# Two attention layers, layer 0: the softmax totals of two head groups made in one visit to TensorE

## Chip, cores and metric

The kernel runs on one core of one Trainium2 chip. The metric is device time in microseconds (us). A comparison uses medians of several runs; the profile is one further execution of the same program.

## What is computed

The input is `x` with shape (8, 512, 32, 32): 8 batch elements, 512 channels, 1024 positions. There are two layers; each normalizes its input by groups of channels and adds an attention block to it. The change is in layer 0 alone:

```python
def _L0_conv_ref(x, gn_w, gn_b, qkv_w, qkv_b, proj_w, proj_b):
    ...                                   # group norm -> normed (b, c, t)
    qkv = jnp.einsum('oc,bct->bot', qkv_w, normed) + qkv_b[None, :, None]
    q, k, v = jnp.split(qkv, 3, axis=1)
    ...                                   # 8 heads of 64 channels, q and k scaled
    weight = jnp.einsum('bct,bcs->bts', q, k)
    weight = jax.nn.softmax(weight.astype(jnp.float32), axis=-1).astype(q.dtype)
    a = jnp.einsum('bts,bcs->bct', weight, v).reshape(b, c, t)
    out = jnp.einsum('oc,bct->bot', proj_w, xf + a) + proj_b[None, :, None]
    return out.reshape(b, -1, h, w)

x = x + _L0_conv_ref(_gn(x), ...)         # layer 0
x = x + _L1_conv_ref(_gn(x), ...)         # layer 1: mixes heads, normalizes the softmax
```

All arithmetic is in fp32. The softmax is made without a maximum: the exponentials `e` are multiplied with `v`, their totals are made on the side, and the product is multiplied with the reciprocals of the totals at the end.

## The kernel before

**Stages.** Layer 0 handles one batch element after the other, up to about 1750 us; layer 1 fills the rest. For each batch element there is an attention loop (some 115 us) and then four projections of 24 us each or less (`k`, `v` and `q` of the next element, the output of this one), each made of seven half-size products by `project0`.

**Groups and slots.** `attention0` works through 8 groups of a batch element. A group `g` is one pair of heads and one of the two blocks of 512 queries. Inside a group, 8 blocks of 128 keys follow, so the loop counter `i` runs over 64 steps, two at a time. For two steps TensorE makes the scores (L1086, into PSUM tile `s`, two buffers), ScalarE the exponentials (L1091, tiles `e`, seven buffers), TensorE the values of the two steps before (L1112, accumulating in the two PSUM tiles `a0` and `a1` of the group), and VectorE adds the exponentials into `zacc` (L1097 for the first addition of a group, L1099 for the others). Each scores or values block of two steps is sixteen matmul records in 64x64 tiles of the TensorE array.

**The end of a group.** After its eighth key block ScalarE copies the two accumulators out (L1123, `u`). Three further steps follow, placed by slot numbers: an `Agenda` is a table from a slot to functions, and the loop runs slots `i` and `i + 1` after the work of step `i`. What is still in the agenda after the loop is run by `ag.flush()`, which stands between the `k` and the `v` projection of the next element.

- `totals`, two slots after the group's end: four matmuls with a block of ones (L1131, tiles of 128x32, eight records) add `zacc` over the partitions into half of a PSUM bank `z`; ScalarE copies that half out (L1136, `row`), and the SP queue moves one row of each 32 to a compact tile `zc` (L1138).
- `reciprocals`, six slots after: VectorE adds the two `u` tiles (L1142), makes the reciprocals (L1145) and two checksums (L1155, L1159); SP writes the reciprocals to DRAM (L1147, `zd`) and reads them back, broadcast over partitions, in two transfers (L1150, `rzb`).
- `finish`, ten slots after: VectorE multiplies and adds into `xa` (L1166, L1168).

`z` takes its PSUM bank from the same tag `a0` (two buffers) that the group accumulators and the single banks of `project0` use.

**What else lies in the slots.** Slots 2 to 8 start `xa`, 4 to 19 hold statistics of the last output and weight combinations, 20 to 38 sums over the next element's channels on ScalarE, 43 and 45 two small matmuls for the group means and squares of the next element (L624, L635, 128x128 tiles), 47 their inverse root on VectorE, 49 to 61 the normalization of the next element on ScalarE, and 32 and 33 the loads of the next left factors. In the last batch element other work takes some of these places: the two small matmuls stand at slots 22 and 25.

**Order.** The program is scheduled by hand (`manual_schedule`): each engine executes in the order in which the code issues, and the SP queue likewise. The pools have fixed buffer counts; `zpool` has two of each tag unless a tile says otherwise, `stat` two.

**In `project0`** the first product goes to two single banks (`a0`), and the products `t6`, `t5`, `t7` to double banks (`s`, two buffers), so `t7` reuses the bank pair of `t6`, which VectorE frees at L933. The last product's two banks are freed by VectorE at L960 for `k` and `q`.

Of the kernel before, what the change touches and what calls it, by code (L numbers as in the profile page):

```python
# [9 lines left out]
F32 = mybir.dt.float32  # L10
# [8 lines left out]
P = 128  # L19
# [448 lines left out]
def tile_two_attention_layers(  # L468
# [19 lines left out]
    nc = tc.nc  # L488
    B, C, T = x_d.shape
# [4 lines left out]
    FB = 512  # L494
# [21 lines left out]
    def const_tile(name, shape, dt=F32):  # L516
        return const.tile(shape, dt, tag=name, name=name)
# [15 lines left out]
    ones = const_tile("ones", [P, P])  # L533
# [165 lines left out]
    with ExitStack() as l0:  # L699
# [4 lines left out]
        zpool = l0.enter_context(tc.tile_pool(name="zpool", bufs=2))  # L704
        stat = l0.enter_context(tc.tile_pool(name="stat", bufs=2))
        ps_s = l0.enter_context(tc.tile_pool(name="ps_s", bufs=2, space=PSUM))
        ps_a = l0.enter_context(tc.tile_pool(name="ps_a", bufs=1, space=PSUM))
# [4 lines left out]
        def score_psum(nm):  # L712
            return ps_s.tile([P, 2, FB], F32, tag="s", name=nm)
# [13 lines left out]
        HC = C // 2  # L727
# [10 lines left out]
        def left_tile(which, b):  # L738
            t = wpool.tile([P, 7, 2, HC], F32, tag="left", name=f"left_{which}_{b}")
            left_t[which] = t  # L740
            return t
# [5 lines left out]
        a21 = {}  # L747

        def load_blocks(which, queue=nc.sync, tag="u0"):

            t = left_tile(which, 0)
            if tag == "junk":
                a21[which] = zpool.tile([P, T], F32, tag=tag, name=f"a21_{which}", bufs=1)[
                    :, :C
                ].rearrange("p (k o) -> p k o", k=2)
            else:
                a21[which] = zpool.tile([P, 2, HC], F32, tag=tag, name=f"a21_{which}")
            for dst, i, j in (
                (t[:, 0], 0, 0), (t[:, 1], 0, 1), (a21[which], 1, 0), (t[:, 2], 1, 1),
            ):  # L760
                for k in range(2):
                    queue.dma_start(
                        out=dst[:, k],
                        in_=SOURCES[which][ts(2 * j + k, P), i * HC : (i + 1) * HC],
                    )
# [13 lines left out]

        load_blocks("k")  # L780
        load_blocks("v")


# [290 lines left out]
        def attention0(b, agenda):  # L1074
            q, k, v = q_t[b], k_t[b], v_t[b]
            e, acc, u, zacc, zc, rzb = {}, {}, {}, {}, {}, {}

            def scores(i):

                f, hp, kc = i // (NG * H // 2), i // NG % (H // 2), i % NG  # L1080
                ps = score_psum(f"s0_{b}_{i}")
                for c in range(2):
                    for m in range(2):
                        r = slice(m * D, m * D + D)
                        k0 = kc * P + c * D
                        nc.tensor.matmul(  # L1086
                            ps[c * D : c * D + D, m], k[r, hp, k0 : k0 + D], q[r, hp, ts(f, FB)],
                            start=True, stop=True,
                        )
                e[i] = epool.tile([P, 2, FB], F32, tag="e", name=f"e0_{b}_{i}")  # L1090
                nc.scalar.activation(e[i], ps, AF.Exp, scale=S0 * S0)  # L1091

            def sums(i):
                g, kc = i // NG, i % NG
                if kc == 1:
                    zacc[g] = zpool.tile([P, 2, FB], F32, tag="zacc", name=f"zacc_{b}_{g}")
                    nc.vector.tensor_add(zacc[g], e[i - 1], e[i])  # L1097
                elif kc > 1:
                    nc.vector.tensor_add(zacc[g], zacc[g], e[i])  # L1099

            def values(i):

                g, hp, kc = i // NG, i // NG % (H // 2), i % NG
                if kc == 0:
                    acc[g] = [
                        ps_a.tile([P, FB], F32, tag=f"a{a}", name=f"a0_{b}_{g}_{a}", bufs=2 - a)
                        for a in range(2)
                    ]
                for a in range(2):
                    rows = slice(a * D, a * D + D)  # L1110
                    for m in range(2):
                        nc.tensor.matmul(  # L1112
                            acc[g][a][m * D : m * D + D], v[rows, kc, ts(2 * hp + m, D)],
                            e[i][rows, m], start=(kc == 0), stop=(kc == NG - 1),
                        )
                if kc == NG - 1:

                    u[g] = [
                        zpool.tile([P, FB], F32, tag=f"u{a}", name=f"u_{b}_{g}_{a}")
                        for a in range(2)  # L1120
                    ]
                    for a in (1, 0):
                        nc.scalar.copy(u[g][a], acc[g][a])  # L1123

            def totals(g):


                HB = FB // 2
                z = ps_a.tile([P, FB], F32, tag="a0", name=f"z_{b}_{g}", bufs=2)[:, :HB]
                for c in range(4):  # L1130
                    nc.tensor.matmul(  # L1131
                        z[c * 32 : c * 32 + 32], ones[:, :32], zacc[g][:, c // 2, ts(c % 2, HB)],
                        start=True, stop=True, tile_position=(0, c * 32),
                    )
                row = zpool.tile([P, HB], F32, tag="row", name=f"row0_{b}_{g}")
                nc.scalar.copy(row, z)  # L1136
                zc[g] = stat.tile([P, T // P], F32, tag="zc", name=f"zc_{b}_{g}")
                nc.sync.dma_start(out=zc[g], in_=row[0::32])  # L1138

            def reciprocals(g):  # L1140

                nc.vector.tensor_add(u[g][0], u[g][0], u[g][1])  # L1142
                zs = zc[g]
                rz = stat.tile([P, T // P], F32, tag="rz0", name=f"rz_{b}_{g}")
                nc.vector.reciprocal(rz, zs)  # L1145
                zd = dram.tile([2, FB], F32, tag=f"zd0_{b}_{g}", name=f"zd0_{b}_{g}")
                nc.sync.dma_start(out=zd, in_=rz)  # L1147
                rzb[g] = zpool.tile([P, FB], F32, tag="rzb", name=f"rzb_{b}_{g}")
                for m in range(2):
                    nc.sync.dma_start(  # L1150
                        out=rzb[g][m * D : m * D + D], in_=zd[m].partition_broadcast(D)
                    )
                col = b * H + g
                junk = stat.tile([P, T // P], F32, tag="junk0", name=f"junkz_{b}_{g}")
                nc.vector.tensor_scalar(  # L1155
                    junk, zs, 1.0, 0.0, ALU.mult, ALU.add, accum_out=chk[:, 1, col : col + 1]
                )
                r2 = stat.tile([P, T // P], F32, tag="r20", name=f"r2_{b}_{g}")
                nc.vector.scalar_tensor_tensor(  # L1159
                    r2, rz, 1.0 / RZ_MAX, rz, ALU.mult, ALU.mult,  # L1160
                    accum_out=chk[:, 0, col : col + 1],
                )

            def finish(g):
                hp, f = g % (H // 2), g // (H // 2)
                nc.vector.tensor_mul(u[g][0], u[g][0], rzb[g])  # L1166
                dst = xa_t[b][:, hp, ts(f, FB)]
                nc.vector.tensor_add(dst, dst, u[g][0])  # L1168


            for i in range(0, NI + 2, 2):
                if i < NI:
                    scores(i)
                    scores(i + 1)
                if i >= 2:
                    for w in (i - 2, i - 1):
                        values(w)
                        sums(w)
                    if (i - 1) % NG == NG - 1:
                        g = (i - 1) // NG  # L1180
                        agenda.at(i + 2, lambda g=g: totals(g))
                        agenda.at(i + 6, lambda g=g: reciprocals(g))
                        agenda.at(i + 10, lambda g=g: finish(g))
                agenda.run(i)
                agenda.run(i + 1)

# [18 lines left out]
        for b in range(B):  # L1205
# [10 lines left out]
            if b < 3:  # L1216

                which = ("k1", "q1", "p1")[b]
# [9 lines left out]
            else:  # L1228
# [11 lines left out]
                for c in range(NCC):  # L1240
                    ag.at(49 + 4 * c, lambda c=c: normalize_to(n_t["1"][:, c], 0, c))
            attention0(b, ag)
            slot = NI + 2
            if more:
# [24 lines left out]
    with ExitStack() as l1:  # L1269
# [5 lines left out]
        zpool = l1.enter_context(tc.tile_pool(name="zpool1", bufs=1))  # L1275
        stat = l1.enter_context(tc.tile_pool(name="stat1", bufs=2))
        ps_a = l1.enter_context(tc.tile_pool(name="ps1_a", bufs=2, space=PSUM))
# [18 lines left out]
        HC = C // 2  # L1296
# [645 lines left out]
        for b in range(B):  # L1942
            more = b + 1 < B
            a = Attention1(b)
# [147 lines left out]
```

## Time and profile before

| | |
|---|---|
| median of 3 runs | 3967.3 us (3964.85, 3967.30, 3968.17) |
| the profiled execution's own time | 3964.89 us |
| its span, first to last instruction | 3963.1 us |
| TensorE clock granted, mean | 0.996 of full |
| TensorE busy | 3874.9 us, 98% |
| VectorE busy | 2769.6 us, 70% |
| ScalarE busy | 1971.4 us, 50% |
| `z` matmuls (L1131) | 512 records |
| `row` copies (L1136) | 64, 0.376 us mean |
| `zc` (L1138), `zd` (L1147), `rzb` (L1150) transfers | 64, 64, 128 |

How to read it: the span is what the trace covers, and the execution's own time is 1.8 us longer. Busy shares are means over both layers. A line such as "L1131 PE MATMUL z<-zacc,ones 128*32 128x256 f32 x8" names the line in the kernel, the engine, the operation, the tile written and those read, the shape of the TensorE tile, partitions times elements, and how many such records were merged; the two numbers ahead of it are the start and the length in us. An entry in square brackets is idle time of the engine just before, and what ended it. TensorE's weight loads have rows of their own (PEld) and overlap the matmuls.

### The profile page before, as it was taken

The numbers are of one execution on the slowest core, as the hardware profiler recorded it, in microseconds if no ns is written. First come the engines' busy times: TensorE is split into PE (matmuls) and PEld (weight loads), VectorE is DVE, ScalarE is ACT, GpSimd is POOL, SyncE is SP. The second block draws the span as 40 slices with busy tenths as digits, with TensorE's granted clock in tenths as the row PEclk, the third lists the DMA queues.
The fourth block names the chain that finished last, engine by engine and source line by source line (L and its number), as shares of the span: only waits on it lengthen the run. The fifth ranks groups of instructions, "written<-read, shape, count | busy, mean of one in ns | idle before, by whom it ended". The sixth has DMA issues, their size and how long they took to land.

```text
span 3963.1 us, 95453 instructions
## 1 busy us (share of the span) xinstructions
PE 3874.9 (98%) x41868; PEld 1823.7 (46%) x41868; DVE 2769.6 (70%) x3741; ACT 1971.4 (50%) x2431; POOL 141.2 (4%) x182
## 2 busy tenths in 40 slices
PE   8999999999999999999999999999999999999997
PEld 4353535344353535344544545545545445445454
DVE  4747475665757474856967958859768679588596
ACT  1726354453627172624716718538347267175284
POOL 0000000000000000000100100001001001000010
PEclk9999999999999999999999999999999999999998
DMA  3313131121121121216938839749568478397494
GB/s 121 123 48 117 47 118 46 55 73 65 55 72 68 61 76 48 89 49 173 230 114 208 211 104 237 198 119 236 158 158 220 134 192 226 98 229 191 124 226 124
DMA packets 249593, 519.09 MB, mean 131 GB/s; under 512 B 51024, under 2 KB 58192, under 8 KB 242512
## 3 DMA queue, kind: packets, MB, share of 16 engines
q1 hardware_dynamic: 241984, 500.08, 44.2%
q0 software_dynamic: 7184, 12.81, 1.5%
q8 instruction: 331, 5.42, 0.6%
q14 instruction: 94, 0.77, 0.1%
HBM read 197.16 MB, written 46.92 MB: 62 GB/s over the span
## 4 chain that ended last, share of the span: by engine, by line
PE 90%; DVE 5%; DMA 3%; ACT 1%; issue 1%; SPq 0%; ACTq 0%; DVEq 0%
PE s L1086 11%; PE a L1112 11%; PE a L1725 11%; PE s L1630 10%; PE m L1667 6%; PE pk_p L904 6%; PE pq_p L904 5%; PE pv L1456 5%; PE pv_p L904 5%; PE pp_p L904 5%; PE pq L1381 4%; PE pp L1381 4%; PE pk L1381 3%; DMA re<-raw 3%; DVE et L1695 1%; DVE bn L1709 1%
## 5 line engine op out<-in xcount | busy, mean ns | idle before, releaser
L1695 DVE STREAM_TRANSPOSE et<-e 128x2048 f32<-128x2048 f32 x256 | 589.5, 2303 | 100.0 <-ACT e L1680 99.0
L1725 PEld LDWEIGHTS a<-et,v 128*64 128x64 f32 x16384 | 510.8, 139 | 296.4 <-issue 273.4
L1709 DVE BATCH_NORM_STATS2 bn<-e 128x6 f32<-128x512 f32 x1024 | 635.1, 681 | 0.0
L1091 ACT ACTIVATE e<-s 128x1024 f32<-128x1024 f32 x512 | 497.2, 1026 | 233.8 <-PE s L1086 233.4
L1642 ACT COPY raw<-s 128x1024 f32<-128x1024 f32 x480 | 470.2, 1018 | 211.6 <-PE s L1630 179.0
L1680 ACT ACTIVATE e<-m 128x1024 f32<-128x1024 f32 x512 | 496.3, 1021 | 156.1 <-issue 56.3
L1725 PE MATMUL a<-et,v 128*64 128x64 f32 x16384 | 558.9, 225 | 11.2 <-DVE et L1695 7.8
L1099 DVE TENSOR_TENSOR zacc<-zacc,e 128x1024 f32<-128x1024 f32 x384 | 468.7, 1221 | 87.8 <-ACT e L1091 65.5
L1630 PE MATMUL s<-k,q 64*64 64x512 f32 x4096 | 515.2, 607 | 5.8 <-DVE q L1496 3.2
L1086 PE MATMUL s<-q,k 64*64 64x512 f32 x4096 | 490.1, 593 | 2.3 <-ACT e L1091 2.3
L1112 PE MATMUL a<-e,v 64*64 64x512 f32 x4096 | 484.1, 589 | 0.0
L1667 PE MATMUL m<-re,wmix 32*32 32x512 f32 x8192 | 311.0, 602 | 19.5 <-DMA re<-raw 16.5
L1112 PEld LDWEIGHTS a<-e,v 64*64 64x64 f32 x4096 | 156.7, 133 | 282.8 <-issue 282.2
L1086 PEld LDWEIGHTS s<-q,k 64*64 64x64 f32 x4096 | 147.9, 133 | 275.2 <-issue 240.5
L1630 PEld LDWEIGHTS s<-k,q 64*64 64x64 f32 x4096 | 127.8, 132 | 220.8 <-issue 87.1
L1456 PE MATMUL pv<-wv,y 128*128 128x512 f32 x480 | 214.3, 599 | 0.0
L1773 POOL DMA_DIRECT2D zd<-rz x96 | 52.5, 552 | 3508.2 <-DVE rz L1767 3506.0
L1741 ACT COPY q<-a 64x256 f32<-64x256 f32 x256 | 94.0, 367 | 148.3 <-PE a L1725 146.2
L1456 PEld LDWEIGHTS pv<-wv,y 128*128 128x128 f32 x480 | 88.6, 190 | 119.8 <-issue 106.5
L1667 PEld LDWEIGHTS m<-re,wmix 32*32 32x32 f32 x8192 | 68.8, 103 | 162.4 <-ACT raw L1642 69.3
L1462 DVE COPY v<-pv 128x512 f32<-128x512 f32 x30 | 20.7, 689 | 159.5 <-PE pv L1456 80.9
L1097 DVE TENSOR_TENSOR zacc<-e,e 128x1024 f32<-128x1024 f32 x64 | 78.3, 1223 | 55.9 <-ACT e L1091 55.9
(317 smaller groups left out, 3866.4 us busy)
## 6 DMA issues: line engine op xcount, KB each, us to landing
re<-raw SPq DMA_DIRECT2D x1024, 256.0 KB
left_q<-left_q SPq DMA_DIRECT2D x17, 1792.0 KB
left_p<-left_p SPq DMA_DIRECT2D x17, 1792.0 KB
left_k<-left_k SPq DMA_DIRECT2D x10, 1792.0 KB
x<-in_x_dram SPq DMA_DIRECT2D x32, 512.0 KB
rzb<-zd SPq DMA_DIRECT2D x128, 128.0 KB
x<-x SPq DMA_DIRECT2D x64, 256.0 KB
y<-x SPq DMA_DIRECT2D x32, 512.0 KB
```

Of the source, the lines that this page charges most:

```text
L904: nc.tensor.matmul(out, st, mv, start=start, stop=(k == 1), skip_group_check=True)
L1086: nc.tensor.matmul(ps[c * D : c * D + D, m], k[r, hp, k0 : k0 + D], q[r, hp, ts(f, FB)], start=True, stop=True,)
L1091: nc.scalar.activation(e[i], ps, AF.Exp, scale=S0 * S0)
L1112: nc.tensor.matmul(acc[g][a][m * D : m * D + D], v[rows, kc, ts(2 * hp + m, D)], e[i][rows, m], start=(kc == 0), stop=(kc == NG - 1),)
L1456: nc.tensor.matmul(ps[:, m], y_t[b][:, c, ts(2 * i + m, P)], w[:, c], start=(c == 0), stop=(c == NCC - 1),)
L1630: nc.tensor.matmul(ps[c * D : c * D + D, m], qo_t[b][r, p, hp, ts(c, D)], k_t[b][r, hp, ts(kh, FB)], start=True, stop=True,)
L1642: nc.scalar.copy(dst, ps)
L1667: nc.tensor.matmul(ps[a // 2][c * 32 : c * 32 + 32, a % 2].rearrange("p (r h k) -> p h r k", r=2, h=2), wmix[rows].rearrange("p g i -> p ( ...
L1680: nc.scalar.activation(e[:, :, 2 * h : 2 * h + 2].rearrange("p r a k -> p a r k"), ps[h].rearrange("p a (r k) -> p a r k", r=2), AF.Exp,)
L1695: nc.vector.transpose(self.et[p, u].rearrange("p kb (r st a) g q -> p st kb r (a g q)", r=2, st=2)[:, st], self.e[p, s].rearrange("p r a ( ...
L1709: nc.vector.bn_stats(self.bn[n][:, p % 2, s, a], e[:, :, a].rearrange("p r k -> p k r"))
L1725: nc.tensor.matmul(acc[two * D : two * D + D, s].rearrange("p (x q) -> p x q", q=4), v_t[b][:, kb, ts(g, D)], et[:, kb, :, g], start=(kb = ...
```

## The change

`totals` is called once for two groups, after the odd one, and makes eight matmuls in place of four: the even group's sums go to the left half of the PSUM bank, the odd group's to the right half. One ScalarE copy takes the whole bank to `row` (now one buffer of 512 columns instead of two of 256); two SP transfers make the two `zc`. `reciprocals` of both groups stand six slots after the odd group's end, `finish` of the even group ten and of the odd group twelve slots after it. So the sums of three groups and the values of three groups can be alive at a time: `zacc` and `u0` get a third buffer, `zc` four. The tile `a21` of the weight blocks shares the tag `u0` and gets the same number.

```diff
-                a21[which] = zpool.tile([P, 2, HC], F32, tag=tag, name=f"a21_{which}")
+                a21[which] = zpool.tile([P, 2, HC], F32, tag=tag, name=f"a21_{which}", bufs=3)
...
-                    zacc[g] = zpool.tile([P, 2, FB], F32, tag="zacc", name=f"zacc_{b}_{g}")
+                    zacc[g] = zpool.tile(
+                        [P, 2, FB], F32, tag="zacc", name=f"zacc_{b}_{g}", bufs=3
+                    )
...
-                        zpool.tile([P, FB], F32, tag=f"u{a}", name=f"u_{b}_{g}_{a}")
+                        zpool.tile([P, FB], F32, tag=f"u{a}", name=f"u_{b}_{g}_{a}", bufs=3 - a)
...
             def totals(g):
                 HB = FB // 2
-                z = ps_a.tile([P, FB], F32, tag="a0", name=f"z_{b}_{g}", bufs=2)[:, :HB]
-                for c in range(4):
-                    nc.tensor.matmul(
-                        z[c * 32 : c * 32 + 32], ones[:, :32], zacc[g][:, c // 2, ts(c % 2, HB)],
-                        start=True, stop=True, tile_position=(0, c * 32),
-                    )
-                row = zpool.tile([P, HB], F32, tag="row", name=f"row0_{b}_{g}")
+                z = ps_a.tile([P, FB], F32, tag="a0", name=f"z_{b}_{g}", bufs=2)
+                for i in range(2):
+                    for c in range(4):
+                        nc.tensor.matmul(
+                            z[c * 32 : c * 32 + 32, ts(i, HB)], ones[:, :32],
+                            zacc[g - 1 + i][:, c // 2, ts(c % 2, HB)],
+                            start=True, stop=True, tile_position=(0, c * 32),
+                        )
+                row = zpool.tile([P, FB], F32, tag="row", name=f"row0_{b}_{g}", bufs=1)
                 nc.scalar.copy(row, z)
-                zc[g] = stat.tile([P, T // P], F32, tag="zc", name=f"zc_{b}_{g}")
-                nc.sync.dma_start(out=zc[g], in_=row[0::32])
+                for i in range(2):
+                    t = zc[g - 1 + i] = stat.tile(
+                        [P, T // P], F32, tag="zc", name=f"zc_{b}_{g - 1 + i}", bufs=4
+                    )
+                    nc.sync.dma_start(out=t, in_=row[0::32, ts(i, HB)])
...
                         g = (i - 1) // NG
-                        agenda.at(i + 2, lambda g=g: totals(g))
-                        agenda.at(i + 6, lambda g=g: reciprocals(g))
-                        agenda.at(i + 10, lambda g=g: finish(g))
+                        if g % 2:
+                            agenda.at(i + 2, lambda g=g: totals(g))
+                            for j in range(2):
+                                agenda.at(i + 6, lambda g=g - 1 + j: reciprocals(g))
+                                agenda.at(i + 10 + 2 * j, lambda g=g - 1 + j: finish(g))
```

More of the change, by code (lines that the diff above doesn't have):

```diff
@@ L1128, in totals @@
                 HB = FB // 2
-                z = ps_a.tile([P, FB], F32, tag="a0", name=f"z_{b}_{g}", bufs=2)[:, :HB]
-                for c in range(4):
-                    nc.tensor.matmul(
-                        z[c * 32 : c * 32 + 32], ones[:, :32], zacc[g][:, c // 2, ts(c % 2, HB)],
-                        start=True, stop=True, tile_position=(0, c * 32),
-                    )
-                row = zpool.tile([P, HB], F32, tag="row", name=f"row0_{b}_{g}")
-                nc.scalar.copy(row, z)
-                zc[g] = stat.tile([P, T // P], F32, tag="zc", name=f"zc_{b}_{g}")
-                nc.sync.dma_start(out=zc[g], in_=row[0::32])
+                z = ps_a.tile([P, FB], F32, tag="a0", name=f"z_{b}_{g}", bufs=2)
[7 more added lines that the diff above has]
+                row = zpool.tile([P, FB], F32, tag="row", name=f"row0_{b}_{g}", bufs=1)
+                nc.scalar.copy(row, z)
+                for i in range(2):
+                    t = zc[g - 1 + i] = stat.tile(
+                        [P, T // P], F32, tag="zc", name=f"zc_{b}_{g - 1 + i}", bufs=4
+                    )
+                    nc.sync.dma_start(out=t, in_=row[0::32, ts(i, HB)])
             def reciprocals(g):
```

## The prediction

> **What bounds the kernel now.** I read the page's first part for the busiest engine, its fourth for the engine that the end hangs on, then the chain in order of time and the timeline around one `totals`.
>
> ```profile
> PE 3874.9 (98%) x41868; PEld 1823.7 (46%) x41868; DVE 2769.6 (70%) x3741; ACT 1971.4 (50%) x2431; POOL 141.2 (4%) x182
> ...
> PE 90%; DVE 5%; DMA 3%; ACT 1%; issue 1%; SPq 0%; ACTq 0%; DVEq 0%
> ```
>
> TensorE holds 90% of the chain. In layer 0's attention it holds all of it. From the chain (start, us, what):
>
> ```profile
> 196.90 1.72 PE a L1112 x16
> 198.61 1.72 PE s L1086 x16
> ...
> 202.62 1.88 PE s L1086 x16
> 204.49 1.72 PE a L1112 x16
> ```
>
> The rhythm is 1.72 us for sixteen matmul records. The gap ahead of 202.62 holds 16 `a` records (1.72) and a `totals` (0.57 by the same view: 202.62 - 202.05). The scores after it take 1.88, not 1.72. So one `totals` costs the path 0.57 + 0.16 = **0.73 us**, and the two starts in the timeline confirm it:
>
> ```profile
> 127.04 1.90 PE L1112 MATMUL a<-e,v 64*64 64x512 f32 x16
> ...
> 128.87 0.64 PE L1131 MATMUL z<-zacc,ones 128*32 128x256 f32 x8
> ...
> 129.44 1.95 PE L1086 MATMUL s<-q,k 64*64 64x512 f32 x16
> 129.57 0.37 ACT L1136 COPY row<-z 128x256 f32<-128x256 f32 x1 [1.08 <-PE z L1131]
> ...
> 131.21 1.90 PE L1112 MATMUL a<-e,v 64*64 64x512 f32 x16
> ```
>
> From 127.04 to 131.21 are 4.17 us; two undisturbed blocks are 3.44. The remainder is 0.73 again, and it is the same to 0.01 us at every `totals` inside the loop.
>
> How much of it is work? `z` streams 256 columns into four column tiles, twice (eight records). A 256-column record elsewhere in this trace (`v0`, chain: 24.44 us for 112 records) takes 0.216 us; four column tiles run at once here (their records start 7 ns apart), so two steps of four are 0.43 us. The other **0.30 us** is the change of tile shape: the first `z` starts 0.52 us after the last `a` where 0.41 would follow, and the steps just after each change are stretched.
>
> ScalarE and VectorE are not the limit there: between 141.8 and 156.2 us they are busy 12.03 and 11.86 of 14.40 us, TensorE all of it. The second place that matters is the flush after the attention, where the last group's totals stand between two projections:
>
> ```profile
> 235.52 0.64 PE L1131 MATMUL z<-zacc,ones 128*32 128x256 f32 x8
> 235.63 0.75 DVE L960 SCALAR_TENSOR_TENSOR k<-pk_p,qkvb,tmp 128x512 f32<-128x512 f32 x1 [0.96 <-PE pk_p L904]
> ...
> 236.43 7.17 PE L904 MATMUL pv_p<-left_v,n 128*128 128x256 f32 x32 [0.27 <-DVE k L960]
> ...
> 243.61 0.69 DVE L1166 TENSOR_TENSOR u<-u,rzb 128x512 f32<-128x512 f32 x1 [4.73 <-DMA rzb<-zd]
> ...
> 247.17 1.22 DVE L933 TENSOR_TENSOR tmp<-tmp,pv_p 128x1024 f32<-128x1024 f32 x1 [2.14 <-PE pv_p L904]
> ```
>
> The last two lines show VectorE standing still for a broadcast to land, and then taking up the projection's work at 247.17, on time.
>
> **What the Trainium skill says.** "TensorEngine Tiling (Array Packing)", Key Properties: changing the tiling mode drains TensorE. The trace agrees: 0.30 us per visit from 64x64 tiles to 128x32 and back. "ScalarE: Activation LUTs", What ACT_TABLE_LOAD costs: an activation is a fixed part plus 0.833 ns an element, so one copy of 512 is cheaper than two of 256. The trace agrees: 0.373 us for 256 (L1136), 0.586 for 512 (L928). "DMA: Bandwidth & Descriptors", Latency and other measured facts: a DMA has a fixed cost near 2 us. The trace: `zc`, issued at 236.62 us, is read at 238.47, 1.85 us later.
>
> **The change, part by part.**
>
> 1. *Totals inside the loop.* Groups 0 to 5 of each of 8 batches: six visits become three, of 16 records each. A visit costs 0.73 for the first eight records and x for the next eight. x is not in the trace. Its floor is the streaming, 0.43; its ceiling is 0.48, if each step keeps the 0.24 us between the first two steps of `z` today. Under 0.43 it can't go, the columns being the same. I take 0.43, since scores also stretch only their first step (0.46, then 0.41). Gain: 24 pairs x (0.73 - 0.43) = **-7.2 us** (-6.0 at the ceiling).
>
> 2. *Groups 6 and 7.* Group 6's visit in the loop (0.73) goes away; both are made in the flush. There TensorE already waits: after `z` it resumes at +0.91 us, when VectorE's last `k` piece frees a bank, and without that wait would resume at +0.57. Eight more records move +0.57 to +1.00, so 0.34 of their 0.43 lies under the wait. Gain per batch 0.73 - 0.09 = 0.64, in seven batches **-4.5**. In the last the wait lasts to +1.28 and covers all: **-0.7**.
>
> 3. *Lost company.* At slot 43 the group-mean matmul (L624) runs right after group 4's totals and costs 0.33 us there; alone, as L635 at slot 45 shows, such a matmul costs 0.47. Group 4's totals move to slot 50, so +0.14 in seven batches: **+1.0**. In the last batch both already stand alone.
>
> 4. *ScalarE.* Two copies of 0.373 become one of 0.586: 0.16 us less per pair. ScalarE is in order, and the exps stand behind the copy; but `z` now lasts 1.16 us and the next scores 0.86 more, so the copy is over before an exp can start. Nothing on the path. Where a copy no longer follows (slots 10, 26, 42, 58) TensorE's 0.73 pause is gone too. The cover for this is the time between the end of an exp and the scores that reuse its bank: 1.2 us as a rule, 0.7 at the tightest, after a group's two `u` copies. Without it TensorE waits for ScalarE, up to 0.3 us a group.
>
> 5. *VectorE and SP.* Per group these are moved, not removed: `reciprocals` (0.68 + 0.20 + 0.11 + 0.08 + 0.17 + 0.08 us on VectorE; `zd` 0.32 and two `rzb` 1.10 on SP), `finish` (0.69 + 0.69), one `zc` (0.58 on SP). Even groups come 8 slots later; odd ones keep their totals and end two slots later. In the loop I cost them at nothing: what VectorE holds back is `e` tiles, and an exp comes 5.9 us or more after the sum that freed its tile. On SP the second `zd` waits behind the first `rzb`, 3 us; behind them stand only prefetches. A visit needs its `zacc` complete; VectorE has less to do just before slots 18, 34 and 50 than now.
>    In the flush the moved work meets the projection. Counting from the start of `z`: copy ends +1.73, first `zc` +1.75, lands +3.6, `zd` +3.8, `rzb` +5.25, second `zd` +6.3, second `rzb` +7.75, landing 3.5 later as now, +11.2; `finish` done at +12.6. L933 stands behind it in VectorE's queue and now starts at +11.65, so it is 0.9 late. It frees the bank of `t6`, which `t7` takes at +14.9; with its 1.22 us it ends at +13.8. Slack 1.1 us, cost nothing. `left_q`, last in that queue, goes 3 us later: it took 7 us from 241.3 and is needed at 260.7.
>
> 6. *Third buffers* (`zacc`, `u0`), four `zc`, one `row`. They let two groups wait together and add no instruction. `row` is rewritten 28 us later. The bank order of `a0` stays such that no `a` waits that doesn't now. Nothing.
>
> **Sum:** -7.2 - 4.5 - 0.7 + 1.0 = **-11.4 us**. Against the profiled execution's 3964.89 (span 3963.1) this is 3953.5. That execution was 2.4 us under the median of the runs shown, 3967.3; from the median: **3955.9 us**. A measurement of this kernel tells about 0.2%, 7.9 us, from no change.
>
> **Rivals.**
>
> A. *The flush chain bites* (slower). If the second `rzb` lands later than +12.3, TensorE waits for L933 in each of 8 batches. At 1.4 us beyond that the gain is gone; at 2.4 us beyond it (+14.7) the kernel is slower by 8 us, 3975. For it: two `zd`-`rzb` round trips in a row, and in one batch today the landing is 0.9 us later than in the others. Against: the transfer engines are 4% busy there. Chance 0.08.
>
> B. *The second eight records pay a change of their own.* x is 0.73: part 1 gives nothing, part 2 about 3 to 4, part 3 takes 1: 3964 to 3965. For it: nothing in the trace has two sets of `z`. Against: same tile shape, and the two steps of `z` today lie 0.24 us apart, so weights load under work. Chance 0.10.
>
> C. *ScalarE takes over in slots 20 to 38*, where the next batch's statistics run on it, with 0.1 to 0.6 us idle per pair of steps. Two or three pairs' gain per batch halves and `u` copies push TensorE: about -7, 3960. Against: the slack of 0.7 us. Chance 0.10.
>
> The change's own forecast: 0.72.
>
> **How the numbers follow.** The likeliest case is 3955.9; with x at its ceiling 3957.1, with medians of runs moving by 2 us either way 3952 to 3959. The range for 8 in 10 takes in C and nearly reaches B: 3951.5 to 3964. Faster by over 0.2% is most of the forecast's own case and half of C: 0.73. Within 0.2%: the rest of it, B, half of C, and the mild end of A: 0.21. Slower: 0.06.
>
> **What would show it.** Right: 24 blocks of 16 `z` records in the loop, each costing the path 1.16 us; 32 copies L1136-like of 128x512 near 0.59 us; the time from flush `z` to the first `pv_p` near 1.0 us; the pair of L624 alone at 0.47; no wait of `pv_p` for VectorE after L933. Wrong: blocks at 1.4 us or more (B), `s` waiting for `e` in the middle of the loop (C), or `pv_p` waiting for `tmp` L933 (A).

## The result, and the profile after

Over 17 runs each the changed kernel takes 3956.74 us in the median, the kernel before 3966.17; these lie 9.4 us apart. The ratio recorded with the runs, which is not the quotient of the two medians, is 0.9983, 95% interval 0.9976 to 0.9990: 6.7 us faster (4.0 to 9.5). A second series (21 runs and 27) gave 3960.70 against 3964.58, ratio 0.9989 (0.9980 to 0.9997), or 4.4 us. The text goes by the ratios: the gain is real, under 0.2%, and about half of the 11.4 us forecast.

The profiled execution took 3963.51 us, only 1.4 less than the one before. To see why, I split each trace at the first scores of layer 1. The timeline has them here, first before, then after:

```profile
1799.05 2.81 PE L1630 MATMUL s<-k,q 64*64 64x512 f32 x24 [1.40 <-DVE v L1044]
```

```profile
1793.99 2.81 PE L1638 MATMUL s<-k,q 64*64 64x512 f32 x24 [1.40 <-DVE v L1044]
```

**Layer 0's length**, from its own first scores (94.79 us before, 95.09 after) to this line, fell from 1704.26 to 1698.90: 5.4 us. (Layer 0's last projection ends at about 1784 us before, later than the 1750 given above, and the length takes in the first projections of layer 1, the same code in both.) What follows this line, again the same code, took 2164.1 and 2167.7. Over the ten traces of this study it lies anywhere between 2156.5 and 2170.1, so layer 0's length is the sharper yardstick, and the experiments below are read by it, part by part. Six of them are one execution each, and their whole times are not compared.

Inside the loop the change does what it was priced at. TensorE's timeline around a pair of totals:

```profile
124.99 1.90 PE L1086 MATMUL s<-q,k 64*64 64x512 f32 x16
126.71 1.90 PE L1114 MATMUL a<-e,v 64*64 64x512 f32 x16
128.54 1.07 PE L1133 MATMUL z<-zacc,ones 128*32 128x256 f32 x16
129.54 1.95 PE L1086 MATMUL s<-q,k 64*64 64x512 f32 x16
131.31 1.90 PE L1114 MATMUL a<-e,v 64*64 64x512 f32 x16
```

From 126.71 to 131.31 are 4.60 us against 3.44 undisturbed: a visit of 16 records costs 1.16, where two visits of eight cost 1.46. All 24 pairs in the loop cost 1.16. The groups by line and shape (busy us, mean ns of one) show the one copy and, in the last row, something new:

```profile
L1133 PE MATMUL z<-zacc,ones 128*32 128x256 f32 x512 | 34.3, 385 | 0.0
L1139 ACT COPY row<-z 128x512 f32<-128x512 f32 x32 | 18.8, 588 | 100.5 <-PE z L1133 100.5
L904 PE MATMUL pv_p<-left_v,tmp 128*128 128x256 f32 x512 | 114.8, 380 | 2.5 <-DVE tmp L933 2.3
```

Before, that `pv_p` row had 0.0 of idle time. TensorE now waits for L933. (The loss is larger than the 2.5 us of this row, which counts idle time from the modelled ends of matmuls; below I go by their starts.) The timeline of the flush shows how (z at 234.56):

```profile
234.56 1.07 PE L1133 MATMUL z<-zacc,ones 128*32 128x256 f32 x16
...
235.56 7.17 PE L904 MATMUL pv_p<-left_v,n 128*128 128x256 f32 x32
...
238.45 0.32 SPq L1153 DMA_DIRECT2D zd<-rz  x1
...
239.85 1.13 SPq L1156 DMA_DIRECT2D rzb<-zd  x2
241.03 0.58 SPq L1153 DMA_DIRECT2D zd<-rz  x1
...
243.57 1.08 SPq L1156 DMA_DIRECT2D rzb<-zd  x2
...
247.16 0.69 DVE L1172 TENSOR_TENSOR u<-u,rzb 128x512 f32<-128x512 f32 x1 [2.27 <-DMA rzb<-zd]
247.88 0.69 DVE L1174 TENSOR_TENSOR xa<-xa,u 128x512 f32<-128x512 f32 x1
248.49 1.21 DVE L933 TENSOR_TENSOR tmp<-tmp,pv_p 128x1024 f32<-128x1024 f32 x1
```

`pv_p` starts 1.00 us after `z`, as forecast. The first round trip `zd` to `rzb` takes 1.40 us on the SP queue, the second 2.54. So the second broadcast lands at +12.6, L933 starts at +13.9 and ends at +15.1, and `t7`, due at +14.9, is late. In this batch element it costs 0.4 us: the next matmul starts 0.29 us late, and the step after it takes 0.10 longer. In the sixth the first round trip already took 3.0 us, and the timeline has

```profile
1316.76 1.21 DVE L933 TENSOR_TENSOR tmp<-tmp,pv_p 128x1024 f32<-128x1024 f32 x1
1318.03 0.70 PE L904 MATMUL pv_p<-left_v,tmp 128*128 128x256 f32 x2 [1.62 <-DVE tmp L933]
```

where 1.9 us are lost. The seven `v` projections lose 4.2 us together, against their 24.28 us each before. The eighth batch element, where a `k` projection of layer 1 stands in this place, loses 0.1: 4.4 in all. The loss follows the transfer exactly: counted from `z`, it is the start of the second `finish` (+12.60 in the fence with `zd`) less 12.21 us. This holds to 0.01 us in all 28 `v` projections of the four runs (this one and three below) in which transfers and `finish` stand as changed.

### The profile page after: what moved, and what is told of

It is laid out like the page before. It is cut to its first block, busy times and chain, and to the rows that moved or that the text cites. A ratio compares the mean times of both kernels' runs of the same rounds, so it can differ in the third digit from the quotient of the medians.

```text
span 3961.7 us, 95330 instructions
## 1 busy us (share of the span) xinstructions
PE 3867.2 (98%) x41868; PEld 1822.7 (46%) x41868; DVE 2768.1 (70%) x3741; ACT 1966.9 (50%) x2399; POOL 140.9 (4%) x182
## 5 line engine op out<-in xcount | busy, mean ns | idle before, releaser
L1733 PE MATMUL a<-et,v 128*64 128x64 f32 x16384 | 556.0, 225 | 10.1 <-DVE et L1703 7.7
L904 PE MATMUL pv_p<-left_v,tmp 128*128 128x256 f32 x512 | 114.8, 380 | 2.5 <-DVE tmp L933 2.3
```

Source lines behind the costliest of these rows:

```text
L1733: nc.tensor.matmul(acc[two * D : two * D + D, s].rearrange("p (x q) -> p x q", q=4), v_t[b][:, kb, ts(g, D)], et[:, kb, :, g], start=(kb = ...
```

## The experiments

**Two visits again.** The pair's second four matmuls stand at slot `i + 4` instead of next to the first four. The function is split: a call makes one half of `z`, and the second call also the copy and the two `zc`.

```diff
-                            agenda.at(i + 2, lambda g=g: totals(g))
+                            agenda.at(i + 2, lambda g=g: totals(g, 0))
+                            agenda.at(i + 4, lambda g=g: totals(g, 1))
```

> The changed kernel, but inside the loop the pair's second four matmuls stand two slots after the first four, so that there are again six visits to TensorE per batch element; copy, row, reciprocals and buffers stay as changed. I read layer 0 as the time from its first scores to the first scores of layer 1: 1704.3 us before, 1698.9 changed. Theory (a visit costs 0.30 us for the change of tile shape and 0.43 for its work): 24 more visits at 0.30, layer 0 near 1706.1, each visit 0.73. Rival (the gain comes from the halved number of ScalarE copies and of their waits): layer 0 stays near 1699.

TensorE's timeline of this kernel:

```profile
126.70 1.90 PE L1114 MATMUL a<-e,v 64*64 64x512 f32 x16
128.52 0.64 PE L1137 MATMUL z<-zacc,ones 128*32 128x256 f32 x8
129.09 1.95 PE L1086 MATMUL s<-q,k 64*64 64x512 f32 x16
130.86 1.90 PE L1114 MATMUL a<-e,v 64*64 64x512 f32 x16
132.69 0.64 PE L1137 MATMUL z<-zacc,ones 128*32 128x256 f32 x8
```

126.70 to 130.86 are 4.16 us: each visit is back at 0.73, with the single ScalarE copy still in place. The loop grows by 0.89 us a batch element, 3 x 0.30, or 7.1 us in eight. Layer 0 came to 1708.9, 2.8 us over what I expected; these lie in the waits behind L933, 1.6 us longer in this execution, and in waits at slots 44 and 46 of two batch elements, 1.2 us. The gain inside the loop is the saved visit and nothing of the copy. That the 0.30 us of a visit belong to the tile shape is read from the starts: scores and values, both in 64x64 tiles, alternate at 1.72 us, four steps of 0.429, with nothing lost between them, while around `z` the step into it is 0.11 us longer than 0.43, the step out of it 0.11 longer than 0.216, and two steps inside are stretched by 0.02 and 0.05. No run here changes the shape alone.

**Both `zd` writes first.**

```diff
                 nc.sync.dma_start(out=zd, in_=rz)
-                rzb[g] = zpool.tile([P, FB], F32, tag="rzb", name=f"rzb_{b}_{g}")
-                for m in range(2):
-                    nc.sync.dma_start(
-                        out=rzb[g][m * D : m * D + D], in_=zd[m].partition_broadcast(D)
-                    )
+                zds[g] = zd
...                                    # broadcast(g) has these lines
+                            for j in range(2):
+                                agenda.at(i + 6, lambda g=g - 1 + j: broadcast(g))
```

> The changed kernel, with the SP queue's order altered: both zd writes of a pair first, then both broadcasts, so that the second round trip no longer waits for the first. Theory (in the flush the second broadcast lands at +12.6 us after z and not at +11.2 as I had it, L933 starts too late, and the third double product waits 0.1 to 1.8 us per batch): the second broadcast lands near +10.3, finish is over near +11.7, and the waits after L933 go: layer 0 falls by about 4.2 us to 1694.7. Rival (it is the amount of moved VectorE work, or the row copy, that makes L933 late): no change, 1699.

The flush in this kernel's timeline (z at 233.84):

```profile
237.72 1.25 SPq L1153 DMA_DIRECT2D zd<-rz  x2
...
239.13 2.41 SPq L1170 DMA_DIRECT2D rzb<-zd  x4
...
244.67 0.69 DVE L1176 TENSOR_TENSOR u<-u,rzb 128x512 f32<-128x512 f32 x1
245.39 0.69 DVE L1178 TENSOR_TENSOR xa<-xa,u 128x512 f32<-128x512 f32 x1
246.00 1.21 DVE L933 TENSOR_TENSOR tmp<-tmp,pv_p 128x1024 f32<-128x1024 f32 x1
```

The four broadcasts go out in one run, the second `finish` no longer waits for its own (in three other batch elements it still waits 0.2 to 0.8 us), and L933 starts at +12.2 instead of +13.9. Layer 0 is 1694.97, 3.9 us shorter; expected were 4.2. The sixth batch element still loses 0.5 us, as its first round trip again took long, 3.5 us. The moved amount of VectorE work and the `row` copy are the same here, so the rival is out.

**`finish` after the projection.**

```diff
-                                agenda.at(i + 10 + 2 * j, lambda g=g - 1 + j: finish(g))
+                                f = lambda g=g - 1 + j: finish(g)
+                                if i < NI:
+                                    agenda.at(i + 10 + 2 * j, f)
+                                else:
+                                    later.append(f)
...
                 v0(b + 1)
+                run_later()
```

> The changed kernel, but the two finish steps of a batch element's last pair are issued after the v projection (in the last batch element after the k projection) instead of in the flush; everything else stays. Theory (VectorE's wait for the second broadcast stands in front of L933): L933 starts at +11.7 us after z as before, no product waits, layer 0 falls by about 4.2 us to 1694.7. Rival (the double product waits for something other than L933, for the reciprocals or a transfer): 1699, with the same gap 14.7 us after z.

Its timeline (z at 234.30):

```profile
243.35 1.08 SPq L1163 DMA_DIRECT2D rzb<-zd  x2
...
246.04 1.22 DVE L933 TENSOR_TENSOR tmp<-tmp,pv_p 128x1024 f32<-128x1024 f32 x1 [6.74 <-PE pv_p L904]
...
260.39 0.68 DVE L1179 TENSOR_TENSOR u<-u,rzb 128x512 f32<-128x512 f32 x1
```

The second broadcast is issued as late as in the changed kernel (+9.05 against +9.01 us), yet L933 starts at +11.74, straight after TensorE, and no projection waits in any batch element. Layer 0 is 1694.60, 4.3 us shorter. It is VectorE's order, `finish` in front of L933, that passes the late landing on to TensorE.

**Two ScalarE steps moved.**

```diff
-                ag.at(2 + 2 * c, lambda c=c: start_xa(b, c))
+                ag.at((2, 4, 6, 10)[c], lambda c=c: start_xa(b, c))
...
-                    ag.at(49 + 4 * c, lambda c=c: normalize0(b + 1, c))
+                    ag.at((49, 53, 59, 61)[c], lambda c=c: normalize0(b + 1, c))
```

> The changed kernel, with two steps of ScalarE moved by two slots: the fourth piece of xa from slot 8 to 10 and the third normalization from slot 57 to 59, so that neither stands in the slot in which a group's two u copies are made. Theory (the 0.10 us that the steps at slots 12 and 60 take beyond the rhythm is TensorE waiting for an exp behind the u copies and this extra activation, which the totals at slots 10 and 58 used to cover): both waits go, 15 x 0.10 = 1.5 us, layer 0 near 1697.4. Rival (the waits belong to the u copies alone): they stay, or move to slots 14 and 62, and layer 0 stays at 1699.

First the kernel before, at the end of group 0:

```profile
113.21 1.94 ACT L1091 ACTIVATE e<-s 128x1024 f32<-128x1024 f32 x2
...
114.41 0.64 PE L1131 MATMUL z<-zacc,ones 128*32 128x256 f32 x8
...
114.97 1.95 PE L1086 MATMUL s<-q,k 64*64 64x512 f32 x16
```

The first of the two exps ends at 114.23 us. The scores that reuse its bank start at 114.97, so the slack is 0.74 us, and 0.73 of it is the `totals` in between. The changed kernel in the same place:

```profile
111.41 1.07 ACT L1125 COPY u<-a 128x512 f32<-128x512 f32 x2 [0.58 <-PE a L1114]
112.37 1.25 ACT L870 ACTIVATE xa<-x,nb,rsy_g 128x1024 f32<-128x1024 f32 x1
112.88 1.90 PE L1114 MATMUL a<-e,v 64*64 64x512 f32 x16
113.51 1.94 ACT L1091 ACTIVATE e<-s 128x1024 f32<-128x1024 f32 x2
...
116.41 1.90 PE L1114 MATMUL a<-e,v 64*64 64x512 f32 x16
```

Two copies and an `xa` piece stand ahead of the two exps, which end at 114.53 and 115.45 us; the scores that reuse their banks follow 0.06 us behind each, at 114.59 and 115.50. From 112.88 to 116.41 are 3.53 us, 0.10 over the rhythm. With the piece moved:

```profile
112.85 1.96 ACT L1091 ACTIVATE e<-s 128x1024 f32<-128x1024 f32 x2
113.36 1.90 PE L1114 MATMUL a<-e,v 64*64 64x512 f32 x16
...
114.67 1.26 ACT L870 ACTIVATE xa<-x,nb,rsy_g 128x1024 f32<-128x1024 f32 x1
...
116.79 1.90 PE L1114 MATMUL a<-e,v 64*64 64x512 f32 x16
```

113.36 to 116.79 are 3.43. The 0.10 is gone at slot 12 of every batch element and at slot 60 of the seven that had it, and comes up nowhere else: 1.5 us. Layer 0 came to 1698.18 and not 1697.4, since in this execution the waits behind L933 were 0.4 us longer and two batch elements waited 0.35 us together at slot 46.

**Six groups paired, two alone.** With `n` = 1, `totals` makes and copies the half of one group.

```diff
-                        if g % 2:
+                        if g > 5:
+                            agenda.at(i + 2, lambda g=g: totals(g, 1))
+                            agenda.at(i + 6, lambda g=g: reciprocals(g))
+                            agenda.at(i + 10, lambda g=g: finish(g))
+                        elif g % 2:
```

> Groups 0 to 5 paired as changed, groups 6 and 7 each with totals, copy, reciprocals and finish of their own at the slots of before. Theory (pairing the last two groups gains 0.64 us per batch at z and loses about as much behind L933): layer 0 is before's 1704.3 less 24 x 0.30, plus 1.0 for the lone mean matmul, plus 0.8 for the wait at slot 12: 1698.9, with no gap behind the flush. Rival (pairing in the flush was worth its 5.2 us): layer 0 near 1704.

Layer 0 is 1699.02; the `v` projections take 24.28 us each as before, and the `totals` at slot 58 cost 0.73 again. Against the first profile of the changed kernel (1698.90), pairing the last two groups therefore brought nothing: the 5.2 us saved at `z` it gave back behind L933 (4.4) and at slot 60 (0.7). Against the second one, below, it cost 3 us.

**Only the buffers.**

```diff
-                    zacc[g] = zpool.tile([P, 2, FB], F32, tag="zacc", name=f"zacc_{b}_{g}")
+                    zacc[g] = zpool.tile([P, 2, FB], F32, tag="zacc", name=f"zacc_{b}_{g}", bufs=3)
...                                    # u0 and a21 three, zc four
```

> The kernel before with only the buffer counts of the change: three zacc, three u0, four zc. Theory (the buffers only let two groups wait together): layer 0 at 1704.3 and every totals at 0.73. Rival (the third buffers relax waits of their own): layer 0 under 1703.

Layer 0 is 1705.45. Every `totals` costs 0.73; two batch elements lost 0.5 and 0.7 us at slot 44. No gain from the buffers alone.

**The changed kernel again**, unaltered, in the second series.

> The changed kernel, unaltered. Its first profile has layer 0 at 1698.9 us (5.4 less than before) and the rest of the span at 2167.7 (3.7 more than before), while the medians of 17 runs differ by 9.4. Theory (layer 1 is the same code and its time scatters by several us from run to run with its transfers): layer 0 within 1.5 us of 1698.9, the rest anywhere from 2156 to 2168. Rival (the change makes layer 1 slower): the rest again near 2167.

The rest of the span was 2165.8, and 2156.5 to 2164.9 in the six kernels above, which contain this same layer 1; before had 2164.1. The traces show no effect of the change on layer 1. Layer 0, though, came to 1702.03, outside the 1.5 us I allowed: its loops are equal to 0.01 us but for one wait of 0.24 at slot 46, and the seven `v` projections lost 6.9 us behind L933 instead of 4.2 (up to 2.0 in one), the `k` projection of the eighth 0.4. The changed kernel's gain in layer 0 is thus itself uneven, 5.4 us in one profile and 2.2 in the other, because a transfer's landing decides it.

**All moves joined** (both `zd` first, `finish` later, the two ScalarE steps), and the group-mean matmul put behind a pair's totals:

```diff
-            agenda.at(slot + 23, gs.means)
+            agenda.at(slot + (23 if b == 0 else 15), gs.means)
```

> The changed kernel with four moves of order and no other work: both zd writes of a pair ahead of the broadcasts; the last pair's finish after the projection that follows the flush; the two ScalarE steps from slots 8 and 57 to 10 and 59; and the group-mean matmul from slot 43 to 35, right behind a pair's totals. Theory: from the changed kernel's 1698.9 us of layer 0 the waits after L933 go (4.3), the waits at slots 12 and 60 (1.5), and the mean matmul costs 0.33 beside the totals and not 0.47 alone (1.0): layer 0 near 1692.1, the whole near 12 us or 0.3% faster than before. Rival (the waits only move, to the later finish, or to the matmul behind slot 35, which needs VectorE's copy of the means): layer 0 at 1695 or more.

The mean matmul in the changed kernel, alone, and then here in company:

```profile
170.24 1.90 PE L1114 MATMUL a<-e,v 64*64 64x512 f32 x16
172.07 0.39 PE L624 MATMUL pm<-gs_m,gavg 128*128 128x4 f32 x2
172.38 1.95 PE L1086 MATMUL s<-q,k 64*64 64x512 f32 x16
174.15 1.90 PE L1114 MATMUL a<-e,v 64*64 64x512 f32 x16
```

```profile
155.14 1.90 PE L1121 MATMUL a<-e,v 64*64 64x512 f32 x16
156.97 1.07 PE L1140 MATMUL z<-zacc,ones 128*32 128x256 f32 x16
157.97 0.39 PE L624 MATMUL pm<-gs_m,gavg 128*128 128x4 f32 x2
158.28 1.95 PE L1093 MATMUL s<-q,k 64*64 64x512 f32 x16
160.05 1.90 PE L1121 MATMUL a<-e,v 64*64 64x512 f32 x16
```

Alone it costs 3.91 - 3.44 = 0.47 us; in company totals and mean together cost 4.91 - 3.44 = 1.47, 0.31 over the 1.16 of the totals. Layer 0 is 1691.93 (1692.1 expected), all projections are equal, and the kernel takes 3952.28 us against 3964.58 before: ratio 0.9970 (0.9958 to 0.9981). In the same series the changed kernel had 3960.70; no interval was taken between these two. The two medians are 8.4 us apart; the two layer 0 lengths of that series differ by 10.1.

## Why the prediction was right, and where it was not

The direction, the range and the mechanism inside the loop held. The size did not: 11.4 us were forecast, and 6.7 and then 4.4 measured by the ratios. Most of the forecast, 0.73, was laid on a gain of over 0.2%, and it was 0.17% and 0.11%. That the first median, 3956.74, lies 0.8 us from the likeliest 3955.9 is luck: layer 0 shows that about half of the gain was lost again, and the second median was 3960.70. By its parts, from the first profile after:

1. *Totals inside the loop*, -7.2: right. x was 0.43, the floor; the steps of `z` lie 0.24, 0.216 and 0.216 us apart. The two-visits kernel gave exactly this sum back.
2. *Groups 6 and 7*, -5.2: right as far as `z`. `pv_p` started at +1.00 and the loop's visit was gone.
3. *Lost company*, +1.0: right. 0.476 alone against 0.315 before (read as 0.33), seven times: +1.1.
4. *ScalarE at nothing*: wrong by +1.5. I named the right cover, 0.7 us of slack after the two `u` copies, and the wait that would come without it, up to 0.3 us a group, but put nothing into the sum. The failing step is the reading of that 0.7. At slot 12 it was 0.74 us, of which TensorE's 0.73 at `totals` were a part, the very pause that the change takes away. The 0.01 us left did not reach: slots 12 and 60, where an activation (1.25 us at slot 12) stands beside the copies, lost 0.10 us each. The slots experiment shows it.
5. *The flush at nothing*: wrong by +4.4 in one profile, +7.3 in the other. The failing term is the second round trip: I put 1.45 us between the second `zd` and its `rzb`, as for a lone one, and it took 2.4 to 2.7 in the two profiles. That used up the slack. What was lost beyond came from the second broadcast's own landing, 3.4 to 5.0 us after its issue where I took 3.5, and in the sixth batch element from the first round trip, 3.0 us. The threshold was right, a landing later than +12.3 where 12.21 was measured; the landing was put at +11.2 and came at +12.3 to +14.2, so the slack of 1.1 us was gone. This is rival A, whose sign, `pv_p` waiting for L933, appeared. I gave it 0.08, mostly as a case that turns the result, and put nothing of it into the sum, where it was a toll of 0.1 to 2.0 us a batch element. "Transfer engines 4% busy" was no argument: it is a mean share, and the cost was the delay of one small write. The trace of before had a warning outside the flush: seven of its 64 trips took 2.4 to 4.0 us, and I took the usual length.
6. *Third buffers*, nothing: right.

The sum with the measured terms is -7.2 - 5.2 + 1.1 + 1.5 + 4.4 = -5.4, and the trace has -5.4. Rival B is refuted by the 1.16 us. Rival C did not come about in slots 20 to 38; its mechanism appeared at slots 12 and 60.

## What to carry to other kernels

When a matmul in another tile shape interrupts TensorE, price the visit and the work apart, and collect what can share a visit: here 0.30 us went with each visit saved, and a third, foreign matmul cost 0.16 us less in company. A step that pauses the bound engine can also be the cover of the others. If it is moved away, take its length off every slack that was measured across it. And where an engine that works in the order of issue gets a step that waits for a transfer, either place it behind the work that the bound engine needs, or issue the transfers so that one round trip does not stand behind another.

## What the runs showed of the hardware that I had not expected

A 4 KB write to DRAM and the broadcast that reads it back were 1.41 us apart on the SP queue (median of 64 before). Seven of these took 2.4 to 4.0 us: the two longest had a load issued some 4 us ahead of them, and four had nothing issued in the 6 us ahead but their own `zc`. For the second of two such pairs, issued right behind the first pair's two broadcasts, it was 2.48 us (median of 32 in the changed kernel, 2.1 to 3.6). With both writes ahead of the broadcasts the second trip no longer delayed TensorE. The first trip in the flush of the sixth batch element took 3.0 to 3.5 us in all seven profiles of kernels that pair the flush, and 1.4 before. What in the path of the transfers makes these differences no run here separates.
